# A 12-stage decoder on one core: where the start-up buffers lie, who makes layer 0's ternary weights, and in how many groups rows are quantized

## The chip, the core and the metric

The kernel runs on one core of a Trainium2 chip. The core has a matrix engine (TensorE; PE in the profile), three engines for element-wise work (VectorE = DVE, ScalarE = ACT, GpSimd = POOL), an engine that mostly issues transfers (SyncE = SP), and 16 DMA engines between the chip's memory and the on-chip memory SBUF. Matmul results land in the accumulator memory PSUM. Each engine works through its own instruction queue in order; engines wait for each other through semaphores. The metric is the device time of one execution in microseconds (us): 1948.71 before, the median of three runs (1945.85 to 1960.44).

## The reference, cut to what matters

A batch of 8 sequences of 128 tokens with 256 features passes through 4 layers. Each layer adds self-attention, cross-attention and a feed-forward block to `x`, each on a layer-normalized `x`. The change lies in layer 0. Its attention has 16 heads of 16 with a causal mask, its cross-attention 32 heads of 8. Its feed-forward block uses quantized linear maps:

```python
def bit_linear(x, w, b):
    gamma_x = clip(max(abs(x), axis=-1), 1e-05)
    x_dq = clip(round(x * 127.0 / gamma_x), -128.0, 127.0) / (127.0 / gamma_x)
    gamma_w = clip(mean(abs(w)), 1e-05)
    w_dq = clip(round(w / gamma_w), -1.0, 1.0) * gamma_w
    return einsum('bsd,hd->bsh', x_dq, w_dq) + b
gate = silu(bit_linear(x, gate_w, gate_b))
val = bit_linear(x, val_w, val_b)
return bit_linear(gate * val, out_w, out_b)
```

So three weight matrices (256 x 1024 each) become ternary, and each token's row is scaled by its own largest value and rounded to an integer. Rounding in the kernel is done by adding and subtracting a large constant (`MAGIC`). A row scaled by 127 over its largest absolute value cannot leave -127 to 127, so the clamps of a row change nothing.

## The kernel before

`decoder` sets up constants and then calls the twelve layer functions in turn. Tokens lie on the 128 partitions, one sequence `b` per slice of the free dimension, so `x` is a tile of 128 x 8 x 256. Functions of layer 0:

- Set-up (L2448 to L2520). `consts`, `x` (two halves of four sequences) and the context `cx` are loaded. Two short-lived pools follow: `start` (L2496), where GpSimd makes a table of -1 (`rows`, L2498) that is written to memory, and `mask` (L2508), where the mask bytes land (`mu`, L2510) and VectorE turns them into floats (L2513). Both pools are opened and closed before the weight pool `wp0` (L2534), on the same side of SBUF, so `wp0`'s buffers lie where these tiles were, and the first load into such a buffer waits until the tile is done with.
- `Ctx.weights` (L96) and `Ctx.stream` (L135) issue weight loads on SP's queue into `wp0`: tiles `w`, `r` and `st` (two buffers each).
- `norm_rows`/`norm_stats` (L140, L144) normalize four sequences: statistics (L155, L156), `var` (L158), Ln and Exp on ScalarE (L125, L126), three small VectorE steps (L129 to L131), then `xn` (L165). `norm` (L172) transposes `xn` on TensorE to `xnT` and adds the output bias to `x` on GpSimd (L184).
- `l0_attn` (L224): projections of q and k in two halves of 512 tokens (L245 to L255, PSUM read by ScalarE at L247, L250 and VectorE at L253), v per sequence (L256), then a software-pipelined loop over the 8 sequences written by `in_step` (L379), in which VectorE masks scores and takes maxima (L280, L285), GpSimd subtracts them (L286), ScalarE exponentiates (L301), TensorE transposes and multiplies.
- `l0_xattn` (L388): the same form with 16 half-sequence units `u`: scores into one PSUM region, copied by ScalarE (L506) into `s` (four buffers), maxima by VectorE (L511), subtraction by GpSimd (L512), Exp (L516), transposes (L358), values (L531), `back` (L364, tile `os`, four buffers), division and projection. The last step adds the result to `x` (L195).
- `l0_ffn` (L583): for the three matrices a sum of absolute values per partition (L599), a matmul with ones for the total (L601), scale and reciprocal (L602, L603), and three VectorE passes of 128 x 2048 to ternary bf16 (L604 to L606, tile `wb`); four pieces of `folds`; the layer norm of all 8 sequences (L618 to L626); the row maxima of all 8 (L632) and three passes per sequence to bf16 `xq` (L640 to L642); transposes to `xqT` (L648). Then a loop over the 8 sequences: a piece of `folds`; two halves of gate and value matmuls, scaled on VectorE (L658, L663), Silu on ScalarE, product `h` on GpSimd (L664); the row maximum of `h` (L667); three passes to bf16 `hq` (L673 to L675); transposes (L679), evacuation by ScalarE and VectorE in turn (L60, L62), the output matmul, and the scaled add to `x` (L683).
- `folds` (L752) is a generator of 12 independent pieces that multiply weight matrices of later layers with each other: loads (L783, L784, L796), transposes (L769), matmuls, copies by ScalarE (L770, L775) and a store (L776) to memory.

The order of instructions within each engine's queue is fixed before the run by a planner: instructions are taken by their place in the program and by when, by its own cost estimates, their inputs are there. Inside `in_step` the written order holds, but instructions from outside, such as the next block's layer norm, are placed between them.

## Time and profile before

| | |
|---|---|
| median of three runs | 1948.71 us |
| the profiled execution | 1957.12 us |
| its span, first to last instruction | 1955.3 us |
| PE busy | 1717.8 us (88%) |
| DVE busy | 1203.0 us (62%) |
| ACT busy | 1037.7 us (53%) |
| POOL busy | 365.8 us (19%) |
| mean granted TensorE clock | 0.939 |

Durations below are from the profiled execution, which took 8.4 us more than the median. "Timeline" rows give start, duration, engine, line, operation, output and inputs with shapes, and in brackets how long the engine had been idle and what it waited for. Rows of "busy time by stretch" give, for each stretch of the span, the busy time and number of instructions of each engine. Rows of the chain give the start, the duration and the engine and line of the work that the end depended on. POOLq, SPq and ACTq are issues of transfers.

### The profile page before, as it was taken

The numbers are of one execution on the slowest core, as the hardware profiler recorded it, in microseconds if no ns is written. First come the engines' busy times: TensorE is split into PE (matmuls) and PEld (weight loads), VectorE is DVE, ScalarE is ACT, GpSimd is POOL, SyncE is SP. The second block draws the span as 40 slices with busy tenths as digits, with TensorE's granted clock in tenths as the row PEclk, the third lists the DMA queues.
The fourth block names the chain that finished last, engine by engine and source line by source line (L and its number), as shares of the span: only waits on it lengthen the run. The fifth ranks groups of instructions, "written<-read, shape, count | busy, mean of one in ns | idle before, by whom it ended". The sixth has DMA issues, their size and how long they took to land.

```text
span 1955.3 us, 25181 instructions
## 1 busy us (share of the span) xinstructions
PE 1717.8 (88%) x9471; PEld 1136.2 (58%) x9477; DVE 1203.0 (62%) x2374; ACT 1037.7 (53%) x1711; POOL 365.8 (19%) x359
## 2 busy tenths in 40 slices
PE   5776977667999986998788989999999997999999
PEld 3453655444666653664466545555555556888667
DVE  4766778856677752326756767677676775454423
ACT  2445854434667741225464377778777763343432
POOL 3543542201121222332002000000000001333200
PEclk9896988878999997998999999999999998999989
DMA  4600026305000022111001110101101004000000
GB/s 135 177 25 1 2 97 209 111 1 215 1 12 6 12 82 105 50 41 51 17 1 36 17 50 18 33 18 34 34 18 34 18 1 162 1 1 1 1 1 22
DMA packets 38970, 90.29 MB, mean 46 GB/s; under 512 B 6865, under 2 KB 19490, under 8 KB 37186
## 3 DMA queue, kind: packets, MB, share of 16 engines
q1 hardware_dynamic: 31266, 69.43, 10.4%
q0 software_dynamic: 5488, 17.67, 3.0%
q8 instruction: 76, 1.25, 0.3%
q10 hardware_dynamic: 2096, 1.57, 0.3%
q14 instruction: 44, 0.36, 0.1%
HBM read 67.15 MB, written 21.51 MB: 45 GB/s over the span
## 4 chain that ended last, share of the span: by engine, by line
PE 68%; DVE 14%; ACT 11%; issue 3%; POOL 2%; DMA 1%; ACTq 0%; DVEq 0%; SPq 0%; POOLq 0%
PE ps_xz L46 9%; PE ps_o L46 7%; PE ps_o L2077 6%; PE ps_o L848 5%; PE ps_mm L46 5%; PE ps_q L46 5%; PE ps_h L46 4%; PE ps_u L46 3%; PE ps_sc L46 3%; PE ps_y L46 2%; PE ps_ty L46 2%; PE ps_xz L1994 2%; DVE mx L511 2%; PE ps_ty L2015 2%; PE ps_sc L209 2%
## 5 line engine op out<-in xcount | busy, mean ns | idle before, releaser
L46 PE MATMUL ps_xz<-xnT,wxz 128*128 128x512 f32 x512 | 237.1, 607 | 0.3 <-ACT ee L1997 0.3
L46 PEld LDWEIGHTS ps_xz<-xnT,wxz 128*128 128x128 f32 x512 | 93.3, 192 | 103.9 <-issue 101.9
L1974 DVE SCALAR_TENSOR_TENSOR xc<-pad,w,xc 128x1024 f32<-128x1024 f32 x96 | 123.1, 1282 | 30.5 <-ACT xc L1968 28.7
L2077 PE MATMUL ps_o<-wo,yg 128*128 128x256 f32 x512 | 128.0, 395 | 1.5 <-DVE yg L2056 1.5
L848 PE MATMUL ps_o<-wvo,uT 128*128 128x256 f32 x512 | 122.6, 383 | 0.0
L848 PEld LDWEIGHTS ps_o<-wvo,uT 128*128 128x128 f32 x512 | 98.5, 193 | 40.7 <-issue 30.3
L1997 ACT ACTIVATE ee<-ps_xz,sgn 128x512 f32<-128x512 f32 x128 | 87.1, 689 | 60.2 <-PE ps_xz L1994 60.2
L2077 PEld LDWEIGHTS ps_o<-wo,yg 128*128 128x128 f32 x512 | 93.5, 192 | 25.4 <-issue 12.9
L2017 DVE TENSOR_TENSOR dtx<-ps_ty,dt 128x512 f32<-128x512 f32 x64 | 41.4, 687 | 90.1 <-PE ps_ty L2015 89.9
L2369 POOL MEMSET gb<- 128x160 f32 x1 | 0.2, 231 | 504.1 <-PE ps_ty L46 504.1
L46 PE MATMUL ps_h<-moe,xT 128*128 x184 | 85.1, 606 | 0.9 <-DVE xT L1244 0.8
L2007 DVE TENSOR_TENSOR ee<-ee,gT 128x2048 f32<-128x2048 f32 x32 | 73.2, 2288 | 8.9 <-ACT ee L2003 8.9
L46 PE MATMUL ps_u<-pT,cx 128*128 128x512 f32 x128 | 70.0, 629 | 6.8 <-ACT pT L831 6.7
L947 ACT ACTIVATE s<-ps_sc,mx,rqs 128x128 f32<-128x128 f32 x128 | 48.1, 456 | 49.5 <-DVE rs_t L129 48.0
L2003 ACT ACTIVATE ee<-ee,sgn 128x1024 f32<-128x1024 f32 x64 | 73.0, 1145 | 0.2
L955 POOL TENSOR_TENSOR s<-s,sums 128x512 f32<-128x512 f32 x32 | 33.3, 1040 | 207.7 <-DVE sums L954 66.6
L512 POOL TENSOR_TENSOR s<-s,mx 128x2048 f32<-128x2048 f32 x16 | 57.8, 3610 | 53.6 <-DVE mx L511 53.6
L1258 DVE TENSOR_TENSOR h<-ps_h,sl 128x512 f32<-128x512 f32 x23 | 15.9, 692 | 82.2 <-PE ps_h L46 82.2
L46 PEld LDWEIGHTS ps_q<-xnT,wqk 128*128 128x128 f32 x512 | 64.3, 199 | 2.8 <-DVE xnT L62 1.0
L46 PE MATMUL ps_q<-xnT,wqk 128*128 128x128 f32 x512 | 64.8, 282 | 0.6 <-DVE xnT L62 0.6
L46 PE MATMUL ps_ty<-ee,dtx 128*64 128x128 f32 x1024 | 63.0, 276 | 2.3 <-DVE ee L2007 2.2
L358 PE MATMUL ps_tr<-consts,s 128*128 128x128 f32 x384 | 55.7, 290 | 8.4 <-ACT s L1726 3.3
(599 smaller groups left out, 4038.3 us busy)
## 6 DMA issues: line engine op xcount, KB each, us to landing
moe<-in_p SPq DMA_DIRECT2D x24, 512.0 KB
rows_in<-zero_rows POOLq DMA_DIRECT2D x1, 8385.0 KB, 34.4
wxz<-in_p9s SPq DMA_DIRECT2D x32, 256.0 KB
fold_vo<-in_p SPq DMA_DIRECT2D x8, 512.0 KB
wvo<-fold_out SPq DMA_DIRECT2D x16, 256.0 KB
wvo<-wvo SPq DMA_DIRECT2D x2, 2048.0 KB
wo<-in_p9s SPq DMA_DIRECT2D x16, 256.0 KB
st<-in_p SPq DMA_DIRECT2D x3, 1024.0 KB
```

Of the source, the lines that this page charges most:

```text
L46: nc.tensor.matmul(out, lhsT, rhs, start=(i == 0), stop=(i == len(pairs) - 1))
L209: k.nc.tensor.matmul(psc(r, n), q[rows], rhs, start=True, stop=True)
L358: k.nc.tensor.transpose(pt[:, r, :], src(g)[:, r, :], k.ident)
L512: nc.gpsimd.tensor_tensor(sv, sv, mx.unsqueeze(2).to_broadcast([P, 16, P]), ALU.subtract)
L848: k.nc.tensor.matmul(self.po[b], uT[:, j, :], self.wvo[:, 4 * hg + j, :], start=hg + j == 0, stop=hg + j == 6)
L947: nc.scalar.activation(s[:, j, :], psc[:, j, :], AF.Exp, scale=rs[:, j : j + 1], bias=mx[:, j : j + 1])
L1974: nc.vector.scalar_tensor_tensor(XC[n], (PAD[n] if n in PAD else pads[n % 2])[:, :, t : t + S], cw[:, n, t : t + 1], XC[n], ALU.mult, ALU.add)
L1997: nc.scalar.activation(e, pm, AF.Relu, scale=sgn[:, at : at + 1])
L2003: nc.scalar.activation(EE[n][:, h], EE[n][:, h], AF.Exp, scale=sgn[:, at : at + 1])
L2007: nc.vector.tensor_tensor(EE[n], EE[n], gT.unsqueeze(1).to_broadcast([P, 2, B, S]), ALU.mult)
L2017: nc.vector.tensor_tensor(DTX[n][:, bs], pt.rearrange("p (b h d) -> p b h d", b=4, d=HD), dt_[:, bs, 2 * n : 2 * n + 2].unsqueeze(3).to_br ...
L2077: nc.tensor.matmul(PO[b // 2][:, b % 2 * D : (b % 2 + 1) * D], YG[n][:, tok(b)], WO[n // 2][:, n % 2, :], start=False, stop=n == 31 and b ...
```

## The change

- The pools `start` and `mask` are taken from the other side of SBUF (`side="right"`); the -1 table is made by ScalarE instead of GpSimd. The activation table for Ln and Exp is asked for once more, at set-up.
- A new function `ternary(k, m, eng)` makes one ternary matrix. For the gate and value matrices it is called in `l0_attn` behind the second half of the q and k projections, with the two scaling passes on GpSimd and the third on ScalarE. `wb` now lies in the weight pool; to make room, `l0_xattn` has three `s` buffers instead of four and two `os` buffers instead of four. The output matrix is made in `l0_ffn`, behind the rows, with its two passes on VectorE and the third on ScalarE.
- In `l0_ffn` rows are normalized by `norm_rows` (Ln and Exp instead of Sqrt) and quantized in two groups of four sequences; the clamps are gone, so that two passes take the place of three, the second over four sequences at once. The four pieces of `folds` and the bias add follow behind.
- In the loop, `hq` takes one VectorE pass and one ScalarE pass instead of three VectorE passes.

```diff
@@ l0_attn, in the loop over the two halves
+            if g:
+                for m in range(2):
+                    ternary(k, m, nc.gpsimd)
@@ l0_xattn
-            s = S_[u] = wk_.tile([P, 4, 4, P], F32, name="s", bufs=4)
+            s = S_[u] = wk_.tile([P, 4, 4, P], F32, name="s", bufs=3)
-            OS[b] = back(k, wk_, PO[b])
+            OS[b] = back(k, wk_, PO[b], 2)
@@ new
+def ternary(k, m, eng):
+    nc = k.nc
+    if m == 0:
+        k.wb = k.wp.tile([P, 3, 2048], BF16, tag="wb", name="wb", bufs=1)
+        k.gam, k.rgam, k.part = (k.sm.tile([P, 3], F32, name=n, bufs=1) for n in ("gam", "rgam", "part"))
+    w = k.stream(k.a["p2"][m])[:, 0:2048]
+    gm, rm, part = (t[:, m : m + 1] for t in (k.gam, k.rgam, k.part))
+    nc.vector.tensor_reduce(part, w, AX.X, ALU.add, apply_absolute_value=True)
+    pg = k.ot((P, 1))
+    mm(nc, pg, [(k.ones, part)])
+    nc.vector.tensor_scalar(gm, pg, 1.0 / (1024 * D), 1e-05, ALU.mult, ALU.max)
+    nc.vector.reciprocal(rm, gm)
+    eng.tensor_scalar(w, w, rm, 1.0, ALU.mult, ALU.min)
+    eng.tensor_scalar(w, w, -1.0, MAGIC, ALU.max, ALU.add)
+    nc.scalar.activation(k.wb[:, m, :], w, AF.Copy, bias=-MAGIC)
@@ l0_ffn: L592 to L606 and L610 to L642 leave; in their place
+        for g in range(2):
+            k.norm_rows(g)
+            gs = slice(4 * g, 4 * g + 4)
+            xn = k.xn[:, gs, :]
+            nc.vector.tensor_reduce(gx[:, gs], xn, AX.X, ALU.max, apply_absolute_value=True)
+            nc.vector.tensor_scalar(gx[:, gs], gx[:, gs], 1e-05, None, ALU.max)
+            nc.vector.reciprocal(sx[:, gs], gx[:, gs])
+            nc.vector.tensor_scalar(sx[:, gs], sx[:, gs], 127.0, None, ALU.mult)
+            for b in range(4 * g, 4 * g + 4):
+                nc.vector.tensor_scalar(k.xn[:, b, :], k.xn[:, b, :], sx[:, b : b + 1], MAGIC, ALU.mult, ALU.add)
+            nc.vector.tensor_scalar(xq[:, gs, :], xn, MAGIC, None, ALU.subtract)
+            for of, m in ((dg, 0), (dv, 1)):
+                nc.vector.tensor_scalar(of[:, gs], gx[:, gs], gam[:, m : m + 1], 1.0 / 127.0, ALU.mult, ALU.mult)
             (the transposes of this group to xqT)
+        k.normed = 0
+        ternary(k, 2, nc.vector)
+        for _ in range(4):
+            next(pieces)
+        for b in range(B):
+            nc.gpsimd.tensor_tensor(x[:, b, :], x[:, b, :], obias, ALU.add)
@@ l0_ffn, in the loop over sequences
-            nc.vector.tensor_scalar(h, h, sh, 127.0, ALU.mult, ALU.min)
-            nc.vector.tensor_scalar(h, h, -128.0, MAGIC, ALU.max, ALU.add)
-            nc.vector.tensor_scalar(hq, h, MAGIC, None, ALU.subtract)
+            nc.vector.tensor_scalar(h, h, sh, MAGIC, ALU.mult, ALU.add)
+            nc.scalar.activation(hq, h, AF.Copy, bias=-MAGIC)
@@ decoder
+    k.exp_table()
-    with tc.tile_pool(name="start", bufs=1) as start:
+    with tc.tile_pool(name="start", bufs=1, side="right") as start:
-        nc.gpsimd.tensor_scalar(
-            rows, k.c[0 : 2 * B, C_ID : C_ID + 2 * B].unsqueeze(2).to_broadcast([2 * B, 2 * B, S]), -1.0, None, ALU.mult
+        nc.scalar.activation(
+            rows, k.c[0 : 2 * B, C_ID : C_ID + 2 * B].unsqueeze(2).to_broadcast([2 * B, 2 * B, S]), AF.Copy, scale=-1.0
         )
-    with tc.tile_pool(name="mask", bufs=1) as start:
+    with tc.tile_pool(name="mask", bufs=1, side="right") as start:
```

## The prediction

> **What bounds the kernel now.** First the timeline of the first 26 us, for what the first matmuls wait for:
>
> ```profile
> 8.36 1.91 DVE L158 TENSOR_SCALAR ln_var<-ln_mv 128x4 f32<-128x4 f32 x1
> 10.68 0.17 DVE L158 TENSOR_SCALAR ln_var<-ln_mv 128x4 f32<-128x4 f32 x1
> 18.89 0.69 DVE L62 COPY xnT<-ps_tr 128x512 f32<-128x512 f32 x1 [0.99 <-PE ps_tr L191]
> 19.50 0.68 DVE L2513 CAST mb<-mu 128x1024 f32<-128x1024 uint8 x1
> 20.21 0.33 SPq L101 DMA_DIRECT2D w<-in_p  x1
> 25.47 16.06 PE L46 MATMUL ps_mm<-xnT,w 128*128 128x512 f32 x32 [6.62 <-DMA w<-in_p]
> ```
>
> The activations (`xnT`) are complete at 19.6. The weights are issued only when the mask's CAST has freed their place, and land at 25.4. Second, the chain that ended last, between the cross-attention's last add (277.9) and the quantized rows:
>
> ```profile
> 279.10 2.46 DVE st L604 x2
> 281.56 1.23 DVE st L605 x2
> 283.74 2.36 DVE wb L606 x2
> 286.25 5.14 DVE xn L624 x8
> 291.41 2.29 DVE gx L632
> 293.69 2.20 DVE part L599
> ```
>
> VectorE alone carries it: ternary weights, then the norm of all eight sequences, then their maxima. The first feed-forward matmul starts at 308.9. Third, busy time by stretch, for cross-attention's loop, the feed-forward's lead-in and its loop (us, then PE, PEld, DVE, ACT, POOL, granted clock, DMA share, GB/s):
>
> ```profile
> 164.00:278.30 114.30, 95.54 (x996) 62.56 (x996) 75.67 (x110) 83.07 (x83) 57.75 (x16) 0.90 0.01 1
> 278.30:309.00 30.70, 18.76 (x77) 14.02 (x78) 27.97 (x60) 9.16 (x17) 5.90 (x8) 0.71 0.83 274
> 309.00:382.00 73.00, 51.62 (x321) 35.39 (x326) 61.70 (x128) 34.22 (x57) 21.83 (x16) 0.88 0.46 162
> ```
>
> VectorE is 91% and 85% busy in the last two; it is their bound. Fourth, groups by line of the feed-forward loop and of GpSimd over the span:
>
> ```profile
> L675 DVE TENSOR_SCALAR hq<-h 128x1024 bf16<-128x1024 f32 x8 | 5.4, 680 | 0.0
> L674 DVE TENSOR_SCALAR h<-h 128x1024 f32<-128x1024 f32 x8 | 5.4, 680 | 0.0
> ```
> ```profile
> L2498 POOL TENSOR_SCALAR less_own_rows<-consts 16x2048 bf16<-16x2048 f32 x1 | 5.4, 5384 | 0.1
> L1079 POOL COPY rt_xr<-rt_xr 128x256 f32<-128x256 f32 x8 | 3.2, 397 | 13.4 <-DVE rt_xr L1074 13.4
> ```
>
> **Part 1, the start.** The weights no longer wait for the mask; SP's queue issues them behind `consts`, at about 1.6 us. They now share the DMA engines with `x` and `cx`. Before, `consts`, `x` and `cx` (2.0 MB) had landed by 9.3, and the second half of `x` by 7.6. With 1.3 MB of `w` and `r` beside them I estimate `x` complete at 9.2 and `cx` at 12.3, `w` about then. TensorE's queue has the transposes of `cx` (1.94) ahead of those of `xn` (1.94); with 0.7 for the copy the first matmul can start near 16.9. If the planner puts `xn` first it is 14.5; if the transfers crowd more, 20. I take 16.5, a gain of **9.0** (5.5 to 11). The first L158 above waits about 1.75 us (1.91 against 0.17) while GpSimd makes the -1 table, 4.85 to 10.2; on ScalarE this goes, as does the 1.28 us table load between Ln and Exp, but transfers cover both, so I count nothing more. The table on ScalarE, about 1.9 us by its 128x2048 copy (L506), runs at 4.6 to 6.5, before Ln is ready. If the transfers weren't late, it would still end first.
>
> **Part 2, ternary in the projections.** VectorE's two sums (2.28 each) already ran at 32.8 to 37.2; that stays. On GpSimd four passes of 128x2048 are new. Nearest row: L1079, one input, 128 partitions; eight times its 0.397 is 3.2, less its start (a one-column TENSOR_SCALAR, L1150, takes 0.22 us) 1.6. The other end is L2498 with 5.4, which writes bf16 on 16 partitions. I take 3.2, being the like row, so 13 us (6 to 22). GpSimd is idle for 22.4 us, from the bias adds' end at 32.7 to its first L286 at 55.08, and the whole stage moves earlier alike: cost 0, at the far end up to 6 if the second `st` lands late. The Trainium skill speaks against the move: "GPSIMD Engine Reference", section 4.1, sends element-wise work to VectorE, though it calls one-input work on GpSimd roughly line-rate. At its two-input 4.5 us (section 3.1; this trace has 3.61 for that, L286) the four would take 18 us, by my row 13; both fit. Queued behind GpSimd's passes are only L286 and, at its third unit, the clearing DMA. ScalarE's two copies to `wb` (1.9 each) wait for GpSimd; behind them in its queue stand L247 and L250, for which PSUM has four buffers. ScalarE is busy 5.9 of 25 us there: 0, at most 6 if the copy is queued before the last of these. The matmul for the total stands in TensorE's queue, and would hold the projections if `st` came late; `st` should land near 20, so 0 to 5. SP's two `st` loads move ahead of the cross-attention's weights, needed 100 us later, and the third waits there until the first `wb` copy frees its buffer, some 40 us in, with only loads needed after 128 behind it: 0.
>
> **Part 3, fewer buffers.** With three `s` buffers, unit t needs that of t-3, whose transposes (L358) TensorE finished in the step before, ahead of scores t in its own queue: 0. `os` of b is read one step after it is written, the next is written two steps after: 0.
>
> **Part 4, work that moves into cross-attention.** The norm and the quantizing of sequences 0 to 3 need nothing later than the fourth sequence's add, at 238.4. The planner will set them between the steps of the loop, as it did for the first half's norm in `l0_attn`, where one step grew from 7.66 to 12.2 us (adds at 92.4, 100.1, 112.3). Moved there on VectorE: variance and small steps 0.7, four `xn` of 0.41, half of L632 1.15, small steps 0.9, four passes of 0.35: 5.8 us. In a 12.0 us pair of steps VectorE is busy 9.5, so 38 us leave it some 8, in scraps; but many of these instructions may stand behind GpSimd. By "SBUF — State Buffer", section "Who interferes with whom", a `tensor_scalar` in VectorE's two-port mode fully blocks behind a running GpSimd instruction; the trace agrees where L158 took 2.75 us at 101.2, against 0.17 as its median, while L286 ran. GpSimd runs 7.1 of 12 us here (L512, 3.61 each). By the rule at its worst thirteen such instructions wait up to 3.6 each, 47 us; by the `l0_attn` case eight instructions lost 3.2 together. I take 4 for waits and 3 for unhidden work or ScalarE's table loads (1.28 each): cost **7** (2 to 14).
>
> **Part 5, the feed-forward block.** From the last add (278.3) to the last scaled add (383.0) it takes 104.7 us. VectorE's work in it was 27.97 + 61.7 = 89.7. Afterwards, behind the add: second half's statistics, Ln/Exp and norm 3.5, maxima 1.65, four passes 1.4, `xq` twice 0.68, `xqT` 0.9, row scales 0.9, output matrix 2.5 (its sum, 2.27, is done earlier, in the projections or the loops): 12.2. The loop loses L674 and L675, 10.8: 50.9. Sum 63.1; at its former share (86%) 73 us. TensorE becomes the rival: 70.4 us of busy time at clocks of 0.71 and 0.88, 59 if all of it scaled with the clock, so about 65; at the share it reached in cross-attention (84%), 77. Both lie close, and each waits for the other, so I take 80: a gain of **24.7** (12 to 32). ScalarE gets 8 copies of about 1.0 and ends at 52 of 80. The bias adds on GpSimd (5.9) wait behind the `folds` pieces and hold only the first L683, far behind.
>
> **Sum.** -9.0 + 0 + 7 - 24.7 = -26.7. The profiled execution (1957.1, its span 1955.3) would become 1930.4; the median of runs was 8.4 lower, so 1922.0.
>
> **The rivals.**
> - *TensorE and `folds` keep the loop's pace.* Twelve pieces stayed queued until 365; four of them ran in the lead-in that goes. Loads and stores are some 13 MB, 48 us at 274 GB/s, and SP issues loads and stores in one queue. If pieces then hold TensorE at 8.6 us a sequence, the block takes 93 instead of 80: 1935. For it: TensorE's 70 busy us; against: in the loop it waits for VectorE (hq L675), not for transfers.
> - *The start stays with transfers.* If `w` and the second half of `x` crowd each other until 22, the gain is 3.5 instead of 9: 1927.5. For it: the DMA engines were full (share 1.00) between 25.5 and 32.7; against: 3.3 MB by 12.3 us is less than the 397 GB/s they then moved.
> - *The lock turns it round.* The thirteen two-port instructions of part 4 and the three small steps with two SBUF inputs each wait a whole L512: 16 x 3.6 = 58, with 3 unhidden, against 33.7 won: 27 slower, 1976. It decides from a mean wait of 1.9 us on. Against it: the 0.4 mean of the like case.
>
> **How the numbers follow.** Forecast 50% (1906 to 1932), loop's pace 22% (to 1943), transfers 12% (to 1936), lock 10% (1949 and above), 6% for better than all this (to 1898). A measurement of this kernel can tell about 1% from no change. Faster by over 1% (below 1929): nearly all of the forecast, half of the transfers' case and the better one, 0.60; slower by over 1% 0.12; between 0.28. Leaving out the lock and the best few per cent, the range is 1904 to 1946.
>
> **What the profile after would show.** First projection matmul at 14.5 to 20, without a wait for `w`. GpSimd's passes near 3.2 us, done before the first L286. Somewhat longer steps behind the fourth sequence's add in cross-attention, with L158-like rows over 1 us. First feed-forward matmul within 15 us of the last add, and the block near 80 us with VectorE and TensorE both over 75% busy. The forecast is wrong if ScalarE or TensorE stand idle for GpSimd in the projections, if the cross-attention loop grows by over 14 us, or if the feed-forward loop keeps 9 us a sequence.

## The result, and the profile after

The changed kernel takes 1980.72 us (median of four runs, 1976.48 to 1981.04), the kernel before 1950.83 beside it (four runs, 1945.85 to 1960.44): a ratio of 1.014, with a 95% interval of 1.010 to 1.0185. The change makes the kernel slower by 1.4%. The forecast was 1922, so it missed the side as well as the size. The profiled execution of the changed kernel has a span of 1978.9 us (1955.3 before) at a mean granted TensorE clock of 0.937 (0.939). The two profiles differ by 23.6 us and the medians by 29.9, because the profiled execution of the kernel before was 6.3 us longer than its median.

Three moments of layer 0, read from the start times of VectorE's adds to `x`, and the end tell where the time went (us):

| | before | after | difference |
|---|---|---|---|
| first add of the attention | 77.06 | 97.86 | +20.8 |
| last add of the cross-attention | 277.89 | 307.72 | +29.8 |
| last scaled add of the feed-forward block | 382.54 | 406.23 | +23.7 |
| end of the span | 1955.3 | 1978.9 | +23.6 |

So the start and the projections lose 20.8 us, the cross-attention 9.4 (the attention's last add is 20.45 later, its share of the 29.8), the feed-forward block gives back 6.1, and nothing changes behind it.

**The start.** The timeline of the kernel before, for the second half of `x` and the context (start, duration, engine, line, what is written and read, and in brackets the idle time before it and what ended it):

```profile
7.62 0.43 DVE L155 BATCH_NORM_STATS2 ln<-x 128x6 f32<-128x256 f32 x1 [0.22 <-DMA x<-in_x]
...
9.35 1.94 PE L219 MATMUL ps_tr<-consts,cx 128*128 128x128 f32 x8 [9.35 <-DMA cx<-in_ctx]
```

That of the changed kernel, for the same two and the first projection:

```profile
16.63 0.43 DVE L155 BATCH_NORM_STATS2 ln<-x 128x6 f32<-128x256 f32 x1 [8.95 <-DMA x<-in_x]
...
21.03 1.94 PE L219 MATMUL ps_tr<-consts,cx 128*128 128x128 f32 x8 [21.03 <-DMA cx<-in_ctx]
...
22.15 0.69 DVE L62 COPY ctxT<-ps_tr 128x512 f32<-128x512 f32 x1 [3.42 <-PE ps_tr L219]
...
28.50 1.92 PE L46 MATMUL ps_mm<-xnT,w 128*128 128x512 f32 x2
```

The weights no longer wait, but `x` does: its second half lands at 16.6 (7.6 before) and the context at 21.0 (9.35). The first projection starts 3.0 us later than before, not 9 earlier.

**The ternary weights.** In the kernel before, GpSimd's first subtraction of row maxima starts here:

```profile
55.08 3.61 POOL L286 TENSOR_TENSOR s<-s,mx 128x2048 f32<-128x2048 f32 x1 [22.35 <-DVE mx L285]
```

The timeline of the changed kernel, from the totals of the two matrices to the first blocks of the attention (the same subtraction is L289):

```profile
44.81 0.50 PE L46 MATMUL ps_o<-part,consts 128*128 128x1 f32 x4
...
45.69 14.33 POOL L599 TENSOR_SCALAR st<-st,rgam 128x2048 f32<-128x2048 f32 x2 [14.80 <-DVE rgam L598]
...
60.00 14.18 POOL L600 TENSOR_SCALAR st<-st 128x2048 f32<-128x2048 f32 x2
67.16 1.91 ACT L601 ACTIVATE wb<-st 128x2048 bf16<-128x2048 f32 x1 [21.36 <-POOL st L600]
69.09 0.33 SPq L137 DMA_DIRECT2D st<-in_p  x1
73.89 2.29 DVE L594 TENSOR_REDUCE part<-st 128x1 f32<-128x2048 f32 x1 [17.73 <-DMA st<-in_p]
...
76.09 2.28 DVE L288 TENSOR_REDUCE mx<-s 128x16 f32<-128x2048 f32 x1
78.28 2.28 DVE L283 TENSOR_TENSOR s<-ps_sc,consts 128x2048 f32<-128x2048 f32 x1
78.45 3.61 POOL L289 TENSOR_TENSOR s<-s,mx 128x2048 f32<-128x2048 f32 x1 [4.27 <-DVE mx L288]
...
80.62 2.09 PE L209 MATMUL ps_sc<-kb,qT 32*128 32x256 f32 x16 [22.33 <-DVE s L283]
```

A pass takes 7.1 us on GpSimd where 3.2 was forecast, and the four begin only at 45.7, because the matmuls for the totals (44.81) stand in TensorE's queue behind all projections of q and k. They end at 74.2, and GpSimd's first subtraction stands behind them. A second wait lies on VectorE: the sum for the third matrix (L594) stands ahead of the first row maximum (L288), and its load was issued (69.09) only when ScalarE had freed the buffer, at GpSimd's pace.

**The cross-attention.** One step, from the add at 258.80 to the next at 280.20, takes 21.4 us; the steps around it take 12.2. Its timeline:

```profile
258.96 3.61 POOL L515 TENSOR_TENSOR s<-s,mx 128x2048 f32<-128x2048 f32 x1 [3.02 <-DVE mx L514]
...
259.93 2.67 DVE L158 TENSOR_SCALAR ln_var<-ln_mv 128x4 f32<-128x4 f32 x1
...
262.86 1.28 ACT L126 ACT_TABLE_LOAD   x1
...
264.98 2.20 DVE L165 TENSOR_SCALAR xn<-x,ln_mv,ln 128x256 f32<-128x256 f32 x4
...
267.22 1.22 DVE L633 TENSOR_REDUCE gx<-xn 128x4 f32<-128x1024 f32 x1
268.35 1.28 DVE L363 COPY pT<-ps_tr 128x512 f32<-128x512 f32 x2
269.09 1.11 PE L361 MATMUL ps_tr<-consts,s 128*128 128x128 f32 x4 [7.55 <-DVE pT L363]
```

The norm and the row maxima of the first four sequences stand in VectorE's queue ahead of the copies (L363) for which TensorE waits 7.55 us. TensorE's granted clock is 0.76 in this step and 1.00 in the steps around it, so a part of the added time may be slower matmuls.

**The feed-forward block.** Busy time by stretch of the changed kernel, for cross-attention's loop, the block's lead-in up to the first feed-forward matmul, and its loop (us, then PE, PEld, DVE, ACT, POOL, granted clock, DMA share, GB/s):

```profile
190.00:308.10 118.10, 94.37 (x984) 62.88 (x984) 82.14 (x129) 84.10 (x84) 60.79 (x20) 0.89 0.00 1
308.10:336.10 28.00, 18.83 (x74) 14.25 (x75) 10.63 (x29) 10.79 (x19) 2.99 (x4) 0.74 0.78 258
336.10:406.70 70.60, 49.61 (x323) 34.40 (x328) 52.93 (x114) 43.83 (x66) 20.82 (x16) 0.94 0.46 155
```

VectorE's work in the block is 10.6 + 52.9 = 63.5 us, and the forecast said 63.1. But the lead-in is still 28 us long, with VectorE idle for most of it, and the loop keeps its pace. The last copy of the quantized rows and TensorE's rows at the end of the lead-in say why:

```profile
320.31 0.59 ACT L60 COPY xqT<-ps_tr 128x512 bf16<-128x512 bf16 x1
...
322.31 3.56 PE L46 MATMUL ps_mm<-fold_vo,fold_vT 128*128 128x256 f32 x8 [2.30 <-DMA fold_vo<-in_p]
...
332.65 3.65 PE L46 MATMUL ps_mm<-fold_vo,fold_vT 128*128 128x256 f32 x8 [3.37 <-DMA fold_vo<-in_p]
...
336.10 1.93 PE L46 MATMUL ps_mm<-wb,xqT 128*128 128x512 bf16 x7
```

The quantized rows were transposed and copied by 320.9, and the matmuls that read them stand behind five `folds` pieces, which wait for their loads: the four called ahead of the loop and the one that the loop's first round calls ahead of its own matmuls. The groups that answer to the loop's row passes shown of before (busy us, mean ns of one, then idle time before):

```profile
L677 ACT ACTIVATE hq<-h 128x1024 bf16<-128x1024 f32 x8 | 8.5, 1060 | 10.3 <-DVE h L676 9.8 <-DVE rs_t L129 0.6
L676 DVE TENSOR_SCALAR h<-h,sh 128x1024 f32<-128x1024 f32 x8 | 6.4, 803 | 0.0
```

### The profile page after: what moved, and what is told of

The parts are those of the page before. It is cut to its first block, busy times and chain, and to the rows that moved or that the text cites. A ratio compares the mean times of both kernels' runs of the same rounds, so it can differ in the third digit from the quotient of the medians.

```text
span 1978.9 us, 25192 instructions
## 1 busy us (share of the span) xinstructions
PE 1713.9 (87%) x9471; PEld 1133.2 (57%) x9477; DVE 1188.7 (60%) x2350; ACT 1057.7 (53%) x1729; POOL 389.3 (20%) x362
## 3 DMA queue, kind: packets, MB, share of 16 engines
q8 instruction: 76, 1.25, 0.3%
## 4 chain that ended last, share of the span: by engine, by line
PE 62%; ACT 9%; DVE 8%; issue 2%; POOL 0%; DMA 0%; DVEq 0%; ACTq 0%; POOLq 0%
PE ps_xz L46 9%; PE ps_o L2079 6%; PE ps_o L46 6%; PE ps_o L850 5%; PE ps_q L46 5%; PE ps_h L46 4%; PE ps_mm L46 4%; PE ps_u L46 3%; PE ps_sc L46 3%; PE ps_y L46 2%; PE ps_ty L46 2%; PE ps_xz L1996 2%; PE ps_ty L2017 2%; ACT sq L2071 1%; PE ps_tr L928 1%
## 5 line engine op out<-in xcount | busy, mean ns | idle before, releaser
L2019 DVE TENSOR_TENSOR dtx<-ps_ty,dt 128x512 f32<-128x512 f32 x64 | 41.4, 687 | 89.9 <-PE ps_ty L2017 89.6
L209 PE MATMUL ps_sc<-kb,qT 32*128 32x256 f32 (+1 forms) x384 | 42.9, 549 | 39.8 <-DVE s L283 24.7
```

The lines of the kernel that those rows point to most:

```text
L209: k.nc.tensor.matmul(psc(r, n), q[rows], rhs, start=True, stop=True)
L2019: nc.vector.tensor_tensor(DTX[n][:, bs], pt.rearrange("p (b h d) -> p b h d", b=4, d=HD), dt_[:, bs, 2 * n : 2 * n + 2].unsqueeze(3).to_br ...
```

## The experiments

The theory after this reading: three separate waits, each made by the place of an instruction in an in-order queue. GpSimd's passes stand ahead of its softmax work, the weights stand ahead of `x` in the DMA engines, and the `folds` pieces stand ahead of the feed-forward matmuls on TensorE. Against it stood, for each, that the wait is only taken up elsewhere. The stages of all runs together, as start times of the same three adds in each run's profile:

| run | first attention add | last cross-attention add | last scaled add | median us | ratio to before (95%) |
|---|---|---|---|---|---|
| before | 77.06 | 277.89 | 382.54 | 1950.83 | |
| after | 97.86 | 307.72 | 406.23 | 1980.72 | 1.014 (1.010 to 1.0185) |
| e1_vec | 86.47 | 295.1 | 395.7 | 1965.66 | 1.008 (1.005 to 1.011) |
| e2_x_first | 91.0 | 300.6 | 399.1 | 1973.07 | 1.011 (1.0075 to 1.014) |
| e3_folds_behind | 97.9 | 307.18 | 393.37 | 1968.40 | 1.009 (1.006 to 1.012) |
| e4_left | 95.25 | 304.59 | 402.98 | 1974.50 | 1.011 (1.008 to 1.014) |
| e6_vec_x_folds | 79.97 | 288.61 | 375.90 | 1946.77 | 0.9975 (0.996 to 0.999) |
| e7_loop_alone | 76.45 | 274.42 | 375.67 | 1950.50 | 0.999 (0.998 to 1.000) |
| e8_table | 76.84 | 284.50 | 371.80 | 1945.62 | 0.997 (0.9955 to 0.998) |
| e9_late | 76.95 | 275.49 | 368.65 | 1943.64 | 0.996 (0.995 to 0.997) |
| e10_split | 71.18 | 308.53 | 395.92 | 1969.03 | 1.008 (1.006 to 1.011) |
| e11_third | 94.42 | 302.95 | 405.67 | 1980.92 | 1.014 (1.012 to 1.016) |
| e12_one_op | 94.96 | 305.52 | 404.54 | 1978.29 (one run) | |
| e13_g0 | 70.05 | 268.49 | 361.52 | 1939.35 | 0.993 (0.990 to 0.995) |
| e16_behind | 99.01 | 309.33 | 374.60 | 1988.44 | 1.0185 (1.015 to 1.022) |
| e17_one_each | 72.45 | 270.92 | 349.43 | 1927.43 | 0.988 (0.986 to 0.991) |
| e18_rows_dve | 71.75 | 270.13 | 355.25 | 1940.54 | 0.993 (0.990 to 0.995) |
| e19_behind_dve | 97.52 | 305.94 | 385.23 | 1995.14 | 1.022 (1.0195 to 1.024) |

The long stages behind layer 0 take a few us more or less from one run to the next, so a run's own effect is read from these columns first. They too differ between profiles of the same code: e6, e8 and e9 are alike up to the cross-attention, and their first adds lie at 79.97, 76.84 and 76.95; before and e7 are alike up to the feed-forward loop, and end the cross-attention at 277.89 and 274.42; the loop of the changed kernel took 55.9 us in its own profile and 57.7 in e1's, where it is the same. So a difference of up to some 3.5 us between two rows, or 2 us in a loop, isn't shown by one pair of profiles.

**e1_vec: the passes on VectorE.**

```diff
-                    ternary(k, m, nc.gpsimd)
+                    ternary(k, m, nc.vector)
```

> After, with the two scaling passes of the first two ternary matrices on VectorE in place of GpSimd; nothing else is touched. Theory (GpSimd's queue): the four passes took 7.13 to 7.16 us each, began only at 45.7 and held GpSimd's first mask subtraction until 78.5 and, through the buffer that they free, VectorE's sum for the third matrix until 73.9. On VectorE four passes are 4 to 5 us, so the first block's adds come 15 to 20 us earlier than in the changed kernel: about 1962 (1959 to 1967), no longer slower than before by over 1%. Rival (the wait is taken up elsewhere: behind the stall TensorE runs at a higher granted clock, and without it the same stage is held by something that comes last anyway, such as the late x): under 6 us, 1975 to 1981.

Measured 1965.66, 15.1 less than the changed kernel; the first attention add comes 11.4 us earlier. The timeline of this run:

```profile
44.42 1.28 DVE L599 TENSOR_SCALAR st<-st,rgam 128x2048 f32<-128x2048 f32 x1
...
46.33 1.22 DVE L600 TENSOR_SCALAR st<-st 128x2048 f32<-128x2048 f32 x1
...
65.09 3.61 POOL L289 TENSOR_TENSOR s<-s,mx 128x2048 f32<-128x2048 f32 x1 [34.48 <-DVE mx L288]
```

A pass costs 1.25 us there against 7.1, and GpSimd reaches its first subtraction 13.4 us earlier. The queue theory holds, though the adds gain 11.4 us and not the 15 to 20 expected; what the medians have beyond that lies behind layer 0. Against the kernel before, 10.0 us of delay of that subtraction remain: about 3 from the start, and about 7 that the passes (5.0) and the third sum (2.3) take on VectorE ahead of the values' copies, for which TensorE waits.

**e2_x_first: x and the context ahead of the weights.**

```diff
-        nc.scalar.dma_start(k.x[:, 4 * g : 4 * g + 4, :], ...)
+        nc.sync.dma_start(k.x[:, 4 * g : 4 * g + 4, :], ...)
-    nc.scalar.dma_start(k.cx, ...)
+    nc.sync.dma_start(k.cx, ...)
```

> After, with the loads of x and of the context moved to SP's queue ahead of the weights. Theory (the order of the transfers): x landed at 16.6 and the context at 21.0 because 6 MB of w, r and st were issued ahead of their second halves; with x first, x is complete near 8 us, the first projection starts at 15 to 20 us in place of 28.5, and the whole is 4 to 12 us shorter only so far as GpSimd's passes move along with it: they hang on the projections through the matmul of the total, so 1969 to 1977. Rival (GpSimd's passes start when their own loads land): the start moves, the first mask subtraction stays at 78, and the time stays at 1979 to 1983.

Measured 1973.07, 7.6 less; the first attention add comes 6.9 earlier. The timeline of this run:

```profile
13.24 2.78 PE L46 MATMUL ps_mm<-xnT,w 128*128 128x512 f32 x4
...
17.92 0.69 DVE L2516 CAST mb<-mu 128x1024 f32<-128x1024 uint8 x1 [5.24 <-DMA mu<-in_mask_BxS_bf]
...
20.54 3.78 PE L46 MATMUL ps_mm<-xnT,w 128*128 128x512 f32 x4 [4.52 <-DVE xnT L62]
```

The first projection starts at 13.2, but the fifth matmul waits for a copy of `xnT` that stands behind the mask's CAST on VectorE, and that CAST waits for the mask to land (17.9). The q and k projections end at 36.3 against 41.4 before: with the order of the transfers mended, the start is worth 5 us, where 9 were forecast.

**e4_left: the pools back in the weights' place.**

```diff
-    with tc.tile_pool(name="start", bufs=1, side="right") as start:
+    with tc.tile_pool(name="start", bufs=1) as start:
-    with tc.tile_pool(name="mask", bufs=1, side="right") as start:
+    with tc.tile_pool(name="mask", bufs=1) as start:
```

> After, with the two temporary pools back in the weights' place, so that the weights are issued behind the mask's CAST again; all else as in the change. Theory (the early weights crowd x and the context out of the queues and so cost more than their wait did): x lands at 7.6 again, the first projection starts at 25 to 26 in place of 28.5, everything behind moves by 2 to 4 us: 1976 to 1979. Rival (the start's edit gains something that the late x only hides): 1981 or more.

Measured 1974.50, 6.2 less than the changed kernel, in runs whose ranges overlap. The timeline of this run shows the wait for the weights restored and the start earlier all the same, so in this kernel moving the pools, which frees the weights, is a loss:

```profile
16.57 0.69 DVE L62 COPY xnT<-ps_tr 128x512 f32<-128x512 f32 x1 [1.09 <-PE ps_tr L191]
...
23.25 3.78 PE L46 MATMUL ps_mm<-xnT,w 128*128 128x512 f32 x4 [6.72 <-DMA w<-in_p]
```

23.25 against 28.50 in the changed kernel and 25.47 before. By the columns the gain is 2.6 to 3.3 us, within the 2 to 4 expected; by the medians it is larger. The 2.2 us against the kernel before lie with the start's other edits (the -1 table on ScalarE, the activation table asked for earlier), which no run took apart. In the trace L158 takes 0.15 us where it took 1.91, no table is loaded between Ln and Exp, and the last copy of `xnT`, which stands ahead of the mask's CAST on VectorE, starts at 16.57 in place of 18.89. The forecast put both at nothing.

**e3_folds_behind: TensorE's order in the feed-forward block.**

```diff
-        for _ in range(4):
-            next(pieces)
         ...
         for b in range(B):
-            next(pieces)
             ...
             nc.vector.scalar_tensor_tensor(x[:, b, :], py, gh, ...)
+            for _ in range(2 if b < 4 else 1):
+                next(pieces)
```

> After, with the first four pieces of the weight folding no longer called ahead of the feed-forward loop; all pieces are called at the end of the loop's rounds, so that the first feed-forward matmuls stand ahead of them in TensorE's queue. Theory (TensorE's order): the quantized rows were turned by 320.9 but the first feed-forward matmul came at 336.1, behind four pieces that wait for transfers; it should now start near 322, and the block from the last cross-attention add to the last scaled add shrinks from 98.5 us to 84 to 90: about 1968 (1964 to 1974). Rival (the total of TensorE's work and of the transfers binds the block: 68 us of matmuls at clocks of 0.74 to 0.92, 13 MB of loads and stores): the pieces are only paid later, in the loop or behind it: 1976 to 1983.

Measured 1968.40, 12.3 less. The timeline of this run:

```profile
309.62 2.78 PE L46 MATMUL ps_mm<-wb,xqT 128*128 128x512 bf16 x8 [0.30 <-ACT xqT L60]
...
317.23 3.78 PE L46 MATMUL ps_mm<-fold_vo,fold_vT 128*128 128x256 f32 x8 [3.98 <-ACT fold_vT L771]
```

The first feed-forward matmul comes 2.4 us behind the last add, where it came 28.4 behind. The block takes 86.2 us instead of 98.5.

**e6_vec_x_folds: the three mends together.** The edits of e1, e2 and e3.

> After, with all three: the first two ternary matrices scaled on VectorE, x and the context loaded ahead of the weights, the folding pieces behind the feed-forward's matmuls. Theory (three separate waits, each in another stage, so their costs add): 1981 less 18, less 9 (the start is worth all of its 8 to 12 us once GpSimd no longer stands behind it), less 12: about 1941 (1930 to 1950), below the kernel before. Rival (one common bound such as the granted clock takes back what the waits gave): 1955 or more.

Measured 1946.77, 34.0 less than the changed kernel; the three alone gave 15.1 + 7.6 + 12.3 = 35.0. The three waits are separate. This version is about as fast as the kernel before, by a ratio of 0.9975.

**e11_third: the third matrix in another buffer.** This takes VectorE's own wait (the sum at 73.89) out of the projections and leaves GpSimd's.

```diff
+    if m == 2:
+        w = k.wp.tile([P, W_COLS], F32, tag="w", name="w")[:, 0:2048]
+        nc.sync.dma_start(w, k.a["p2"][m][:, 0:2048])
+    else:
-    w = k.stream(k.a["p2"][m])[:, 0:2048]
+        w = k.stream(k.a["p2"][m])[:, 0:2048]
```

> After, with the third ternary matrix loaded into a buffer of the weights in place of the second stream buffer, so that its sum stands behind the cross-attention in VectorE's queue and no longer waits there, at 73.9, for GpSimd to free a buffer. Theory (two waits in a row: GpSimd's own queue until 74.2, and VectorE's sum that held the first row maximum until 78.4): only the second goes, the first block's adds come 4 to 5 us earlier (the first near 93.5 in place of 97.9), and the whole is 2 to 5 us shorter unless the later sum costs the feed-forward's lead-in the same: 1976 to 1981. Rival (VectorE's wait is the whole stall): the first add near 80, the whole near 1963.

```profile
73.41 7.17 POOL L289 TENSOR_TENSOR s<-s,mx 128x2048 f32<-128x2048 f32 x2
```

GpSimd's first subtraction now follows its last pass at once, at 73.41 in place of 78.45, the first attention add comes 3.4 us earlier, and the feed-forward block takes 4.2 us more: 1980.92 in all. Of the stall in the projections, GpSimd's queue is the bulk and VectorE's wait 3 to 5 us.

**e12_one_op: the price of a GpSimd pass.**

```diff
-    eng.tensor_scalar(w, w, rm, 1.0, ALU.mult, ALU.min)
-    eng.tensor_scalar(w, w, -1.0, MAGIC, ALU.max, ALU.add)
+    eng.tensor_scalar(w, w, rm, None, ALU.mult)
+    eng.tensor_scalar(w, w, MAGIC, None, ALU.add)
```

> After, with one arithmetic operation in each of the four GpSimd passes (a multiplication, then an addition); the clamps to -1 and 1 are left out, so the matrices are not ternary where a weight exceeds the mean by more than half again. If GpSimd's price goes by operations: about 3.6 us a pass, as one-input work of one operation by the row that the prediction took, the totals to the first mask subtraction 14 us shorter. If it goes by elements alone: 7.1 us a pass as before.

This kernel leaves out the clamps to -1 and 1.

```profile
46.08 10.89 POOL L599 TENSOR_SCALAR st<-st,rgam 128x2048 f32<-128x2048 f32 x2 [15.47 <-DVE rgam L598]
56.96 10.73 POOL L600 TENSOR_SCALAR st<-st 128x2048 f32<-128x2048 f32 x2
```

Neither expectation: in this run's timeline a pass with one operation takes 5.4 us, with two 7.1. That is the 5.38 us of the row L2498 of the kernel before, which has the same 2048 columns and one operation on 16 partitions: in these rows the price goes by the operations and not by the partitions. No run varies the columns.

**e7_loop_alone: the loop's edit in the kernel before.**

```diff
-            nc.vector.tensor_scalar(h, h, sh, 127.0, ALU.mult, ALU.min)
-            nc.vector.tensor_scalar(h, h, -128.0, MAGIC, ALU.max, ALU.add)
-            nc.vector.tensor_scalar(hq, h, MAGIC, None, ALU.subtract)
+            nc.vector.tensor_scalar(h, h, sh, MAGIC, ALU.mult, ALU.add)
+            nc.scalar.activation(hq, h, AF.Copy, bias=-MAGIC)
```

> The kernel before with one edit of the change: in the feed-forward loop a sequence's rows are scaled and rounded by one VectorE pass and turned to whole numbers by ScalarE, where three VectorE passes stood. The two clamps are left out as in the change; they cut off nothing that a row scaled by its own maximum can reach. The prediction (VectorE's 61.7 us in the loop set its pace): the loop's 57.7 us from the first scaled add to the last fall by 8 to 11, so 1943 to 1946. Theory now (a sequence takes some 8 us because it is a chain through five engines, with a folding piece in TensorE's queue, and no engine is full): two of the three passes were on the chain, but ScalarE's pass with its wait takes nearly as long, so 0 to 3 us are gained: 1949 to 1954.

Measured 1950.50, a ratio of 0.999 (0.998 to 1.000). From the first to the last scaled add 56.1 us against 57.7 before, with VectorE's work in that stretch down from 51.4 to 43.5 us. The largest single term of the forecast is worth 1.5 us in the loop where it was put, which is no more than two profiles of one loop differ by.

**e16_behind and e19_behind_dve: no piece in the loop.** First all twelve pieces are called behind the loop; then, in that version, the rows are quantized by three VectorE passes again.

```diff
-        for _ in range(4):
-            next(pieces)
         for b in range(B):
-            next(pieces)
             ...
+        for _ in range(12):
+            next(pieces)
```

> After, with all twelve folding pieces called behind the feed-forward loop, so that no piece stands among its matmuls in TensorE's queue; all is computed. Theory A (TensorE's queue: a piece of about 4 us with its own waits for ScalarE stands in every sequence's way): first to last scaled add falls from 55.9 us to under 42, that is under 6 us a sequence, and the pieces then take 40 us or more behind it; the whole is slower than the version with the pieces at the loop's rounds, 1975 to 2000. Theory B (the chain of one sequence through VectorE, ScalarE, GpSimd, VectorE, ScalarE, TensorE sets the pace): 7 to 8 us a sequence remain, 49 us or more, and the whole is 2000 or more.

> The version with all twelve pieces behind the loop (e16), with the rows quantized by three VectorE passes as in the kernel before. Theory (VectorE, busy 34.8 of 39.5 us there, is the loop's bound once no piece stands in it): the 42.1 us from the first to the last scaled add grow by 7 to 10, to 49 to 52, and the whole by as much: 1995 to 1999. Rival (the chain through the engines): under 3 us more, 1988 to 1991.

Busy time from the first to the last scaled add, of e16 and then of e19:

```profile
332.46:374.60 42.14, 25.95 (x178) 16.05 (x180) 36.12 (x88) 22.24 (x31) 14.64 (x12) 1.00 0.16 50
```
```profile
331.35:385.23 53.88, 36.34 (x197) 22.36 (x196) 44.89 (x102) 17.47 (x27) 14.91 (x11) 0.84 0.19 60
```

Without pieces a round takes 6.0 us instead of 8.0, and VectorE is busy 86% of it. With the three passes back, VectorE has 8.8 us more to do and the loop grows by 11.7. This fits a bound by VectorE that the pieces hid. The granted clock differs too (1.00 and 0.84), and what part of the 11.7 belongs to it these two runs can't say. In all the time grows from 1988.44 to 1995.14, and both are slower than the changed kernel: in e16 the loop ends 31.6 us earlier, but behind the twelve pieces the next layer's first add comes at 451.3, 11.0 later than in the changed kernel.

**e8_table and e9_late: the norm inside the cross-attention.** Both start from e6. The first loads ScalarE's table ahead of the loop (`k.exp_table()` in front of `in_step`). The second keeps the norm of the first four sequences behind the loop:

```diff
+        eps = k.sm.tile([P, 1], F32, name="eps", bufs=1)
+        nc.vector.tensor_scalar(eps, x[:, 7, 0:1], 0.0, 1e-05, ALU.mult, ALU.add)
         for g in range(2):
-            k.norm_rows(g)
+            k.norm_rows(g, eps)
```

> The version with all three mends (e6), with ScalarE's table for Ln and Exp together loaded once ahead of the cross-attention's loop, so that the norm of the first half, which runs inside that loop, needs no table of its own. Theory A (table loads: the step that takes 21.4 us in place of 12.2 holds two of 1.28 us each, in front of the loop's own Exp and copies): 2.5 to 4 us less, 1943 to 1944.5. Theory B (the lock: VectorE's norm and quantizing instructions wait for GpSimd's running subtraction, and ScalarE has room): under 1 us, 1946 to 1948.

> The version with all three mends (e6), with the variance of the first four sequences made to depend on the last one's add (its small constant is worked out from that row, times zero), so that their norm and quantizing stay behind the cross-attention's loop, as in the kernel before. If moving them is worth its place: the loop ends 8 to 9 us earlier, the feed-forward's lead-in grows by the 5.8 us of VectorE work and the wait for Ln and Exp, and as the folding pieces no longer stand in front, all of this is on the path: 0 to 4 us slower or faster than e6, 1944 to 1951. If the lock and the tables cost more than the work itself: 4 us or more faster, under 1943.

With the tables gone the long step takes 20.1 us instead of 21.4, and the whole 1945.62 instead of 1946.77: the two loads cost 1.3 us of the 9.2 that this step takes beyond the 12.2 of the others, between the two expectations. In e9 every step is 12.2 us, the cross-attention is 9.4 us shorter, the block behind it takes 93.2 us instead of 87.3, and the whole is 1943.64, between the two ranges. Moving the norm into the loop is a loss of about 3 us: VectorE's 5.8 us of instructions saved 5.9 behind the loop and cost 9.2 in it, with their waits and the tables, because they stand in its queue ahead of copies that the loop's chain needs.

**e10_split: the passes in the attention's loop.** From e6, one of the four VectorE passes at the end of each of four steps.

```diff
+            (2, lambda b: passes[b]() if b < 4 else None),
```

> The version with all three mends (e6), with the four scaling passes of the first two ternary matrices on VectorE in the first attention's loop, one at the end of each of four steps, where in e6 they stood ahead of the values' copies in the projections. Theory (the passes, 5.0 us, and the third matrix's sum, 2.3, held the values' PSUM buffers: 16.3 us from the totals to the first mask add, against 9.0 before): the projections give back 5 to 7 us, the loop takes back 0 to 3, since VectorE stands idle 6.7 us in it: 1940 to 1944. Rival (the loop's step is bound by VectorE and takes all of it back): 1945 to 1948.

Measured 1969.03, 22 us worse than e6, against both expectations. The timeline of this run:

```profile
71.09 3.61 POOL L288 TENSOR_TENSOR s<-s,mx 128x2048 f32<-128x2048 f32 x1 [5.91 <-DVE mx L287]
...
71.52 4.26 DVE L604 TENSOR_SCALAR st<-st 128x2048 f32<-128x2048 f32 x1
...
89.43 2.29 DVE L594 TENSOR_REDUCE part<-st 128x1 f32<-128x2048 f32 x1 [13.09 <-DMA st<-in_p]
```

Two things happened. Beside a running subtraction three of the passes take 4.3, 4.6 and 4.6 us instead of 1.25, and the first, beside GpSimd's issue of a transfer (57.77 to 60.71), takes 3.1: each ends 1.0 to 1.1 us behind GpSimd's instruction. And the sum for the third matrix waits at the head of VectorE's queue for 13 us, since its buffer is freed later. In the projections themselves the split did what it should: the first attention add is at 71.2, 8.8 earlier than in e6 and 5.8 earlier than in e9.

**e13_g0: the passes under the projections.** From e9, the ternary call behind the first half of the q and k projections.

```diff
-            if g:
+            if not g:
                 for m in range(2):
                     ternary(k, m, nc.vector)
```

> The version e9 (all three mends, and the norm of the first four sequences behind the cross-attention), with the first two ternary matrices called after the first half of the q and k projections in place of the second, still on VectorE. Theory (the passes cost what they hold up: in e9 they stand before the values' copies, which free TensorE's PSUM buffers; some 6 us earlier VectorE is idle beside TensorE's projections): the 5 us of passes go under them, 1937 to 1941. Rival (the totals' matmuls now stand in the middle of TensorE's projections and wait there for the sums, which end at 29.9): the gain is eaten, 1942 to 1946.

Measured 1939.35. The timeline of this run:

```profile
30.93 2.48 DVE L599 TENSOR_SCALAR st<-st,rgam 128x2048 f32<-128x2048 f32 x2
...
33.33 2.36 DVE L600 TENSOR_SCALAR st<-st 128x2048 f32<-128x2048 f32 x2
```

All four passes lie at 30.9 to 35.7, beside TensorE's projections and with no GpSimd work near, and the first attention add is at 70.05: 6.9 earlier than in e9, and 7.0 earlier than in the kernel before. As far as the first add tells, the passes cost nothing here, as the forecast had it for GpSimd.

**e17_one_each and e18_rows_dve: one piece behind each round.** From e13, which has two pieces behind each of the first four rounds, one piece behind each round and the last four behind the loop; then the same with three VectorE passes for the rows (the edit of e7 undone).

```diff
-            for _ in range(2 if b < 4 else 1):
-                next(pieces)
+            next(pieces)
+        for _ in range(4):
+            next(pieces)
```

> The version e13 with one folding piece in each of the loop's eight rounds and the last four behind the loop, where e13 has two in each of the first four rounds and one in the others. Theory A (a piece in the way costs a round some 3 us): the first four rounds fall from 10 us to 8, the block ends 6 to 10 us earlier, and the four pieces behind it take back 6 to 14 us, so 1938 to 1948. Theory B (the rounds are paced by their own chain): the rounds stay as they are and the four pieces come on top, 1948 or more.

> The version e17 with the loop's rows quantized as in the kernel before: three VectorE passes in place of one and ScalarE's copy. Theory (with the pieces spread, VectorE is what a round waits for; the loop's edit was right but had no effect while the pieces held TensorE): the loop's 48.8 us grow by 5 to 10, 1932 to 1938. Rival (the loop's edit is worth nothing anywhere): within 2 us of e17, 1926 to 1930.

e17 measured 1927.43, a ratio to before of 0.988 (0.986 to 0.991), the best of all and better than either expectation: 1.2% faster than the kernel before, and by the medians 2.7% faster than the changed one. Its block takes 78.5 us (93.0 in e13), near the 80 of the forecast. Its loop, and then that of e18:

```profile
300.61:349.43 48.82, 40.84 (x273) 28.43 (x274) 40.76 (x95) 32.88 (x54) 15.23 (x12) 1.00 0.56 176
```
```profile
301.43:355.25 53.82, 42.82 (x264) 30.07 (x265) 47.92 (x105) 25.34 (x45) 17.05 (x12) 0.94 0.48 153
```

In e13 the loop takes 65.2 us, also at a granted clock of 1.00, so each of the four pieces cost some 4 us in it. Behind the loop, where e17 has them, they take most of that back: its loop ends 12.1 us earlier than e13's, the next layer's first add only 1.6. The rest of e17's lead builds up behind, most of it, 9 us, in the last 120 us of the span, where the same work ran at a granted clock of 1.00 in e17's profile and 0.92 in e13's. What set that clock isn't settled, so of the 11.9 us between the two versions only a small part is shown to come from the edit. In e18 the loop takes 53.8 us instead of 48.8, with 7.2 us more work for VectorE: the loop's edit is worth up to 5.0 us once each round's piece stands behind its matmuls, though the granted clock differs here too (1.00 and 0.94). The whole, 1940.54, is above what was expected and again has the slower end.

## Why the prediction was wrong, step by step

By the profiles the forecast's -26.7 us became +23.6. The start missed by 12.5 us (at the first mask add), the ternary passes by 17.3, the cross-attention by 2.4 and the feed-forward block by 18.6. Besides the price of a GpSimd pass, the three large misses have one form: the forecast read how long an engine is busy or idle, and not what stands ahead of an instruction in its queue or beside a load in the DMA engines.

- **What bounds the kernel.** The shares of VectorE were read rightly (91% and 85%), and its work afterwards was forecast as 63.1 us and measured as 63.5. The failing inference was that the block's time follows that share: it took 98.5 us where 80 was forecast.
- **Part 1, the start: -9.0 forecast, +3.0 measured** (25.47 to 28.50). The failing step is the estimate of `x` complete at 9.2 and `cx` at 12.3. It counted only the 1.3 MB of `w` and `r` beside them, but SP's queue then holds two `st` loads of 1 MB each and the next `w` and `r` as well, and `x` landed at 16.6, `cx` at 21.0. A second, smaller term: from the context's landing to the first projection 4.6 us were counted (1.94 + 1.94 + 0.7), and it took 7.5. VectorE's copy of the context (L62, 22.15) stands in its queue ahead of the norm's last steps, and one `xn` pass took 2.08 us in place of 0.41 while GpSimd was at work. The rival "the start stays with transfers" had the mechanism, but its worst case was still a gain; e2 and e4 show the loss. The Trainium skill, page "DMA: Bandwidth & Descriptors", section "Queues, rings and completion order", says that each DMA engine takes turns between its queues; this fits a small load on ScalarE's queue that has to share with a long row of loads on SP's: moved to the head of SP's own queue, the two landed at 7.7 and 9.6 (e2).
- **Part 2, ternary on GpSimd: 0 forecast, with a far end of 6; +17 measured** (the stage's 20.8 less the start's 3.5 at the first mask add). Two terms failed. The price, 3.2 us a pass, came from a COPY (L1079); the row named as the other end, L2498 with 5.4, was the true neighbour for one operation (e12), and two operations take 7.1, above the range's upper end of 22 us for the four (28.5). And the cover: the 22.4 us of GpSimd's idle time were counted from 32.7, but the matmuls for the totals stand behind the projections, so the passes could begin only at 45.7. The first subtraction would have been due at 58.5 (the mask add at 53.86 and its maximum, 2.3 us each), which leaves 12.8 us of cover: just enough at 3.2 a pass, 15.7 short at 7.1. Named in the forecast as a place where the totals could hold TensorE ("0 to 5"), this queue held GpSimd instead. The third matrix's load was put at 0 because only later loads stand behind it; its sum stands in VectorE's queue ahead of the first row maximum, and that cost 3 to 5 (e11).
- **Part 3, fewer buffers: 0, no sign against it**; no run tried it alone.
- **Part 4, work moved into the cross-attention: +7 forecast, +9.4 measured.** Right in mechanism and place (the step behind the fourth add). The mis-sized term is the "3 for unhidden work": the lock caught one instruction (L158, 2.67 instead of 0.17), the tables cost 1.3, and most of the 5.8 us of VectorE work was on the chain. That it isn't worth its place, e9 shows.
- **Part 5, the feed-forward block: -24.7 forecast, -6.1 measured.** The failing step is "both lie close, and each waits for the other, so I take 80": the order in TensorE's queue was left out. The four pieces stand behind the rows, but ahead of the first feed-forward matmul in TensorE's queue, with the loop's first piece behind them (28 us instead of "within 15"); e3 took 12.3 us back. In the loop a piece ahead of every round's matmuls hid the 8 us that VectorE lost: 1.5 alone (e7), up to 5.0 with the piece behind the matmuls (e18), at most 11.7 with none (e19). The rival "folds keep the loop's pace" was right in mechanism, and its 93 us for the block was near the 98.5.
- **The rival that ended on the other side** gave 1976, and 1980.7 was measured, but not by its mechanism: in the changed kernel the lock cost about 2.5 us in the cross-attention, and 1.7 in the start if the slow `xn` pass is one. It took e10 to show it at work. The number was met by chance.
- **What the profile after would show.** Of the three signs of being wrong the first came true: in the projections ScalarE stood idle for GpSimd (21.36 us at L601), and TensorE at GpSimd's pace (22.33 us at L209, released by VectorE, whose queue waited for the third matrix). The other two did not: the cross-attention grew by 9.4 us, not by over 14, and the feed-forward loop kept 8.0 us a sequence (8.2 before), not 9. Of the rest, the first projection had no wait for `w`, but started at 28.5, not at 14.5 to 20, and L158 rose over 1 us (2.67), as forecast.

## What to carry to other kernels

Before work is given to an idle engine, look up when its input is released in the queue of the engine that makes it, and price it from a row of the same operation, with the same number of operations and columns; an idle time counts only from that moment. When an engine's busy time falls and the stage doesn't, read the other engines' queues for what stands ahead of the next stage's first instruction: moving the lines that call independent work was worth 12 us here. Before a transfer is freed to start early, look for what is needed sooner and shares the DMA engines with it: here the first projection came 3.0 us later for it.

## What the runs showed that was not expected

- A GpSimd `tensor_scalar` of 2048 columns took 5.4 us with one operation and 7.1 us with two, on 128 partitions, and 5.4 us with one on 16 partitions. VectorE took 1.25 us for the same pass. The Trainium skill, "GPSIMD Engine Reference", section 4.1, calls one-input work on GpSimd roughly line-rate; here it was about four to six times VectorE's time, and the measurement decides.
- VectorE's 1.25 us pass took 3.1 to 4.6 us when GpSimd was at work as it was issued (e10), and ended 1.0 to 1.1 us behind GpSimd's instruction. The Trainium skill, "SBUF — State Buffer", section "Who interferes with whom", says that such a pass in VectorE's two-port mode fully blocks; these rows agree with it, where the like case of before had shown a mean wait of 0.4.
- With the same work, the last 120 us of the span took 118.5 us before (from the add at 1833.6 to the last at 1952.0), 121.4 in e13 (clock 0.92) and 112.1 in e17 (clock 1.00). No run here tells what sets that clock.
